# A two-layer graph attention kernel: a new table of places, transfers modelled kind by kind, and one sum kept in a slot of `x`

## The chip, the cores and the metric

The kernel runs on one core of one Trainium2 chip. The metric is the device time of one execution in microseconds (us). The time before is the median of three executions, 2783.31 us (2777.88 to 2784.37). A core has a TensorE (PE, matrix products), a VectorE (DVE), a ScalarE (ACT), a GpSimd (POOL) and a SyncE (SP). Each runs its own list of instructions strictly in order and waits at the head of that list for the semaphores of other engines. Here SP does nothing but issue transfers (DMAs), POOL issues the transfers that add to what is in their destination, and ACT and DVE share the elementwise work.

## The reference, cut to what matters

For each of 32 graphs of 512 nodes with 512 features, the layer normalizes the features, applies a relu, and runs two graph attention layers: the first with 4 heads of 256 features, the second with one head of 512. The result is added to the input.

```python
def gat_layer(x, mask, W, a_src, a_dst, bias, concat):
    B, N, _ = x.shape
    H, F = a_src.shape
    xl = (x @ W).reshape(B, N, H, F)
    asrc = jnp.einsum('bnhf,hf->bnh', xl, a_src)
    adst = jnp.einsum('bnhf,hf->bnh', xl, a_dst)
    e = jax.nn.leaky_relu(asrc[:, :, None, :] + adst[:, None, :, :], NEG_SLOPE)
    e = jnp.where(mask[..., None], e, NEG_INF)
    attn = jax.nn.softmax(e, axis=1)
    out = jnp.einsum('bsdh,bshf->bdhf', attn, xl)
    ...

h = jnp.maximum(_layernorm(x, axis=-1), 0.0)
# gat: layer 1 (concat, elu), layer 2 (mean over one head)
x = x + gat(adj, h, W1, att_src1, att_dst1, b1, W2, att_src2, att_dst2, b2)
```

All of it is float32. For one graph the products with weights are 512x512 by 512x1024 (layer 1) and 512x1024 by 1024x512 (layer 2), and the attention products are 512x512 by 512x256 for each of four heads and 512x512 by 512x512 for the second layer.

## The kernel before, in words

**Products.** Each of the four products of a graph (`project1`, `gather1`, `project2`, `gather2`) is cut into 2x2 blocks and done with seven block products in place of eight. That needs sums of blocks of the left and of the right operand, which DVE makes (`sums`, `sums1`, `sums2`), and sums of the seven results, which ACT and DVE make when they take a result out of its PSUM bank. There are eight banks. A block product is one job on PE of two or four matmuls of 256 to 258 columns. One of the seven products of `project1` (number 5, `SMALL`) is itself cut in seven, with matmuls of 129 columns (`step`). A matmul in float32 shows as two matmul records in the trace.

In `sums` the four sums of the left operand are `s1`, `s2`, a sum in place, and `s4`. In `project1`, `s4` has a tile of its own, `hs4`, which product 3 of all four quarters of the result reads. In `gather1` of the last turn (order `SINGLY`) `hs4` holds the fourth sums too. `x` has four slots (`xs`): a graph's four input tiles lie there from their load to the end of `norm_turn`, and `sums2` takes three of them for right operands of `gather2`.

**Turns.** The main loop has 31 turns. Turn i does the first attention product of graph i+1, the second layer's softmax and attention product of graph i, `project1` and the first layer's softmax of graph i+2, `project2` of graph i+1, and loads and normalizes graph i+3. Before the loop lie the loads of weights, their scores (`scores1`), graph 0 and `project1` of graph 1.

**A softmax in this kernel** goes through DRAM twice for each pair of heads. `columns` computes per-node scores; `spread` turns them on DVE, writes 4 KB to DRAM (`das<-as`), and reads them back onto all partitions (`as<-das`, 512 KB). `first` reads `as` with one ACT instruction (`l<-as,z`) for each of four tiles, adds the transposed mask on DVE, takes exponentials on ACT, and spreads the sums the same way (`drr<-rr`, `rr<-drr`). `second` builds the probabilities in `p`, has POOL add the mask from DRAM (`p<-dm`), and takes exponentials on ACT.

**What sets the order.** No instruction is emitted when its line of the kernel runs. `Program.add` records a job with its engine, its cost in us, the keys it reads and writes, and for a transfer a size. `Program.ranks` gives every job a rank from the table `PLACES` (in hundredths of a us, one number for every job ahead of the loop, of one turn and of the last turn; later turns add the PE work of a turn). `Program.order` then plays five engines in order and two transfer queues ("wires", SP's and POOL's): whenever an engine is free it takes, of the jobs whose inputs the model holds to be ready, the one with the lowest rank. The order found is the order in which each engine's instructions are emitted; costs, sizes and places have no other effect. In this model a transfer starts `DMA_LEAD` after its issue, takes its size in us, slowed by a share in `SHARED` when both queues are busy, and is known to have landed `DMA_TAIL` later.

```python
if len(busy) == 2:
    speed["SP"], speed["POOL"] = self.SHARED.get(jobs[wires["SP"][0][0]][4], (0.4, 0.6))
...
    release(j, lambda s: event + self.DMA_TAIL[which])
```

**Where the recorded lines are.** The helpers that record (`act`, `dve`, `dma`, `accumulate`, `pe`) have one line each, so the profile shows nearly all of ACT at L495, DVE at L498, SP at L501, POOL's transfers at L506 and PE at L512. Tiles tell the work apart.

Of the kernel before, what the change touches and what calls it, by code (L numbers as in the profile page):

```python
# [10 lines left out]
F32 = mybir.dt.float32  # L11
# [8 lines left out]
P = 128  # L20
# [24 lines left out]
class Banks(Slots):  # L45
# [314 lines left out]
def tile_gat(  # L360
# [616 lines left out]
    M = N // 2  # L977
# [713 lines left out]
```

## Time and profile before

| what | value |
|---|---|
| median of three executions | 2783.31 us |
| lowest and highest | 2777.88 and 2784.37 us |
| the profiled execution's own time | 2778.11 us |
| its span, first to last instruction | 2776.3 us |
| PE busy | 2747.9 us |
| DVE busy | 2561.7 us |
| ACT busy | 2224.7 us |
| POOL busy | 321.7 us |
| share of 16 DMA engines' span, SP's queue and POOL's | 42.4% and 25.1% |

The span is the time from the first to the last instruction; 1.8 us of the profiled execution's time lie around it. Busy time is the union of an engine's instructions; matmuls overlap one another in the records, since the next one starts while the one before drains. The views of waits give, for an engine and a tile, what ended its idle time, in us in total, how many times, and the longest. A timeline row gives start, length, engine and tile, how many instructions were merged, and in brackets the idle time before it.

### The profile page before, as it was taken

How to read it: one execution, taken by the hardware profiler on the slowest of the kernel's cores; microseconds unless marked ns; L12 is line 12 of the kernel's file. 1: busy time of each engine (PE TensorE's matmuls, PEld its weight loads, DVE VectorE, ACT ScalarE, POOL GpSimd, SP SyncE). 2: the span in 40 equal slices, each digit the busy share in tenths (PEclk: the TensorE clock that was granted, in tenths of full speed). 3: DMA queues.
4: the chain of work that ended last, by engine and by line, in shares of the span. 5: the costliest groups of instructions: out<-in, count | busy, mean ns of one | idle time of the engine just before them, and what ended most of it. 6: DMA issues, size and time to landing. Idle time of an engine off the chain costs nothing. (4 is left out here: it accounts for less than half of the span.)

```text
span 2776.3 us, 42499 instructions
## 1 busy us (share of the span) xinstructions
PE 2747.9 (99%) x12924; PEld 2375.5 (86%) x12924; DVE 2561.7 (92%) x6732; ACT 2224.7 (80%) x4907; POOL 321.7 (12%) x356
## 2 busy tenths in 40 slices
PE   7999999999999999999999999999999999999999
PEld 6688888888888888888888888888888888888887
DVE  7899999999999999999999999999999999999996
ACT  5978788788887787887888877878778788778783
POOL 0101111101111111111011111111111111101110
PEclk9999999999999999999999999999999999999999
DMA  7757766767666767667686666766666766677663
GB/s 224 182 146 180 199 177 173 199 172 201 175 179 180 187 177 199 178 175 195 170 206 174 175 184 174 191 190 176 178 194 172 203 173 172 194 168 201 165 159 117
DMA packets 375865, 502.15 MB, mean 181 GB/s; under 512 B 222804, under 2 KB 227668, under 8 KB 375636
## 3 DMA queue, kind: packets, MB, share of 16 engines
q1 hardware_dynamic: 329844, 332.68, 42.4%
q0 software_dynamic: 45792, 166.74, 25.1%
q8 instruction: 103, 1.69, 0.3%
q14 instruction: 126, 1.03, 0.1%
HBM read 316.41 MB, written 51.31 MB: 132 GB/s over the span
## 5 line engine op out<-in xcount | busy, mean ns | idle before, releaser
L512 PE MATMUL mm<-w_sb,hs 128*128 128x257 f32 (+3 forms) x2908 | 675.8, 368 | 12.8 <-ACT xl L495 5.9
L512 PEld LDWEIGHTS mm<-w_sb,hs 128*128 128x128 f32 x2908 | 540.1, 190 | 93.3 <-ACT xl L495 8.9
L506 POOL DMA_DIRECT2D p<-dm x314 | 273.5, 877 | 2328.9 <-DVE p L498 1095.2
L512 PE MATMUL mm<-w_sb,ht 128*128 128x258 f32 x2112 | 522.8, 382 | 0.1
L512 PE MATMUL mm<-p,xl 128*128 128x258 f32 (+1 forms) x1984 | 493.1, 383 | 1.5 <-ACT mm L495 0.8
L512 PE MATMUL mm<-w_sb,h 128*128 128x257 f32 x2056 | 487.2, 379 | 0.2 <-ACT mm L495 0.2
L498 DVE SCALAR_TENSOR_TENSOR p<-rr,z 128x512 f32<-128x512 f32 (+1 forms) x636 | 447.4, 742 | 4.6 <-DMA rr<-drr 4.4
L512 PEld LDWEIGHTS mm<-w_sb,ht 128*128 128x128 f32 x2112 | 394.5, 190 | 58.0 <-issue 0.7
L495 ACT ACTIVATE p<-p,z 128x512 f32<-128x512 f32 (+1 forms) x636 | 428.2, 713 | 19.6 <-DVE p L498 13.0
L512 PEld LDWEIGHTS mm<-w_sb,h 128*128 128x128 f32 x2056 | 389.3, 189 | 58.2 <-ACT mm L495 0.6
L512 PEld LDWEIGHTS mm<-p,xl 128*128 128x128 f32 x1984 | 365.1, 190 | 61.2 <-issue 5.5
L495 ACT ACTIVATE l<-l,low 128x512 f32<-128x512 f32 x516 | 369.7, 717 | 1.9 <-DVE low L498 1.6
L495 ACT ACTIVATE l<-as,z 128x512 f32<-128x512 f32 x516 | 353.2, 715 | 14.6 <-DMA as<-das 14.3
L498 DVE CUSTOM_DVE_ANT_1 l<-l,mt 128x512 f32<-128x512 f32 x516 | 345.3, 688 | 18.1 <-ACT l L495 12.7
L495 ACT ACTIVATE xl<-mm 128x258 f32<-128x258 f32 (+2 forms) x748 | 274.2, 376 | 81.5 <-PE mm L512 80.2
L495 ACT ACTIVATE mm<-mm 128x257 f32<-128x257 f32 (+2 forms) x498 | 169.8, 345 | 203.3 <-PE mm L512 108.4
L495 ACT ACTIVATE h<-mm,b_sb 128x256 f32<-128x256 f32 (+1 forms) x504 | 227.8, 473 | 121.5 <-PE mm L512 121.0
L512 PE MATMUL mm<-t,hs 128*128 128x258 f32 (+1 forms) x992 | 254.7, 380 | 0.0
L512 PEld LDWEIGHTS mm<-t,hs 128*128 128x128 f32 x992 | 183.6, 190 | 24.0 <-DVE xl L498 0.4
L495 ACT ACTIVATE xr<-h 128x512 f32<-128x512 f32 x256 | 159.7, 625 | 45.5 <-DVE h L498 42.8
L512 PE MATMUL mm<-xl,p 128*128 128x258 f32 (+3 forms) x752 | 190.0, 388 | 0.0
L498 DVE TENSOR_TENSOR xl<-xl,mm 128x258 f32<-128x258 f32 x372 | 155.7, 420 | 36.2 <-PE mm L512 31.7
(137 smaller groups left out, 3752.6 us busy)
## 6 DMA issues: line engine op xcount, KB each, us to landing
p<-dm POOLq DMA_DIRECT2D x314, 512.0 KB, 5.0
rr<-drr SPq DMA_DIRECT2D x159, 512.0 KB
x<-in_x_dram SPq DMA_DIRECT2D x129, 256.0 KB
adj<-in_adj_dram SPq DMA_DIRECT2D x128, 256.0 KB
as<-das SPq DMA_DIRECT2D x64, 512.0 KB
t<-in_x_dram SPq DMA_DIRECT2D x124, 256.0 KB
out_dram<-t SPq DMA_DIRECT2D x124, 256.0 KB
dm<-m SPq DMA_DIRECT2D x64, 256.0 KB
```

The costliest lines, as they stand in the source:

```text
L495: prog.add("ACT", cost, reads, writes, lambda: nc.scalar.activation(*a, **k))
L498: prog.add("DVE", cost, reads, writes, lambda: f(*a, **k))
L506: lambda: nc.gpsimd.dma_start(to, at, accum_op=OP.add), size,
L512: f(*a, **k)
```

## The change

Six things change; the jobs, their engines and their instructions stay the same.

1. All of `PLACES` is replaced.
2. A transfer's lead, tail and the two shares of speed are looked up by its size in a table `KIND` (`MASK` for POOL's), in place of one lead and tail for each queue and a table of shares.
3. Sizes of transfers in the model change: loads of `x` and masks 0.93 to 0.76, loads of weights 0.93 to 0.89 (and 1.5 to 1.78 for a block of the second weights), stores 0.77 to 0.70, POOL's additions 2.35 to 2.14, transposes 1.25 to 0.97, mask stores 0.80 to 0.73, the 4 KB writes 0.10 to 0.25, the spread rows 1.16 and 2.32 to 0.79 and 2.28.
4. The cost of a small product of 129 columns goes from 129/593 to 129/576 us.
5. The tile `hs4` is gone. In `sums` of `project1`, `s4` takes a slot of `x`, given back when `project1` ends; the four `x` slots so serve eight takers in a turn in place of seven.
6. In the last turn's `gather1`, the fourth sums of all heads take halves of one slot of `x`, given back at its end.

```diff
 PLACES = (
-    -54128, -54128, -54128, -54317, -50216, -53799, -49031, -53371, -49031, -48940, -49031, -48940, -5322, 4139,
...
+    39933, 29566, 31469, 32046, 32674, 28922, 29748, 26576, 30181, 34026,
 )
...
-    DMA_LEAD, DMA_TAIL, AHEAD = {"SP": 0.45, "POOL": 0.42}, {'SP': 1.2, 'POOL': 1.15}, 3.5
-    SHARED = {0.93: (0.31, 0.7), 0.77: (0.43, 0.71), 2.32: (0.75, 0.31), 1.16: (0.75, 0.31), 1.25: (0.35, 0.57)}
+    AHEAD, MASK, OTHER = 3.5, (0.69, 1.16), 0.76
+    KIND = {
+        0.25: (0.65, 0.33, 0.08, 0.89),
+        0.7: (0.18, 0.97, 0.18, 0.84),
+        0.73: (0.14, 1.23, 1.0, 0.59),
+        0.76: (0.91, 0.87, 0.36, 0.59),
+        0.79: (1.9, 0.76, 0.49, 0.45),
+        0.89: (0.65, 1.5, 0.11, 0.87),
+        0.97: (-0.2, 1.07, 0.21, 0.52),
+        1.78: (0.65, 1.5, 0.11, 0.87),
+        2.28: (0.6, 0.96, 0.58, 0.4),
+    }
...
+    def kind(self, j):
+
+        if self.jobs[j][0] == "POOL":
+            return self.MASK
+        return self.KIND.get(self.jobs[j][4], self.KIND[self.OTHER])
...
-                speed["SP"], speed["POOL"] = self.SHARED.get(jobs[wires["SP"][0][0]][4], (0.4, 0.6))
+                speed["SP"], speed["POOL"] = self.kind(wires["SP"][0][0])[2:]
...
-                release(j, lambda s: event + self.DMA_TAIL[which])
+                release(j, lambda s: event + self.kind(j)[1])
...
-                wires[e].append([j, free[e] + self.DMA_LEAD[e], jobs[j][4]])
+                wires[e].append([j, free[e] + self.kind(j)[0], jobs[j][4]])
...
-    hs4 = sbuf.tile([P, KQ, N // 2], F32, name="hs4")
...
-    XLOAD, STORE, MASKS, TURN, MASK_OUT, SMALL_ONE = 0.93, 0.77, 2.35, 1.25, 0.8, 0.1
-    ROWS = {4: 1.16, 8: 2.32}
+    XLOAD, WLOAD, STORE, MASKS, TURN, MASK_OUT, SMALL_ONE = 0.76, 0.89, 0.7, 2.14, 0.97, 0.73, 0.25
+    ROWS = {4: 0.79, 8: 2.28}
...
-            s4 = (hs4, [("hs", 2, 0), ("hs", 2, 1)]) if kh == KQ and at == 0 else s2
+            s4 = s2
+            if kh == KQ and at == 0:
+                xk, xt = xs.take()
+                s4 = xt[:, : KQ * M].rearrange("p (k m) -> p k m", m=M), [xk]
...
+            if place is None:
+                left["own"] = xk
...
-                akeys + bkeys + ([tk + (1,)] if q == 1 else []), [bk], w / 593,
+                akeys + bkeys + ([tk + (1,)] if q == 1 else []), [bk], w / 576,
...
+        xs.give(left["own"])
...
-        ahead = {h for h, n in order[:2]}
+        ahead, apart = {h for h, n in order[:2]}, None
+        if order is SINGLY:
+            xk, xt = xs.take()
+            apart = xk, xt[:, : 2 * M].rearrange("p (i f) -> p i f", i=2)
+            for i in range(2):
+                prog.alias(xk + (i,), [xk])
...
+        if apart:
+            prog.alias(xk, [xk + (i,) for i in range(2)])
+            xs.give(xk)
```

Built, both programs hold the same instructions on each engine. On PE a job moves by at most 17 places in the order, most by four or fewer; on DVE most move by ten or fewer.

More of the change, by code (lines that the diff above doesn't have):

```diff
@@ L594, in weights1 @@
                     dma(
-                        XLOAD, (), [("w1", ix, k)], w1_sb[:, ix, k, :, 2:],
+                        WLOAD, (), [("w1", ix, k)], w1_sb[:, ix, k, :, 2:],
                         w1[row : row + P, :].rearrange("p (j c f) -> p c j f", j=H // 2, c=2)[:, c],
@@ L604, in scores1 @@
                 dma(
-                    0.75, (), [vk + ("v", a, j)], bc[:, 2 * a + j, :],
+                    XLOAD, (), [vk + ("v", a, j)], bc[:, 2 * a + j, :],
                     bass.AP(tensor=v.tensor, offset=v.offset + j * 2 * FH, ap=[[0, P], [1, 2 * FH]]),
@@ L631, in weights2 @@
             dma(
-                1.5, [("ht", 0, 0)], [("w2", ix)], w2_sb[:, ix, :, :M],
+                2 * WLOAD, [("ht", 0, 0)], [("w2", ix)], w2_sb[:, ix, :, :M],
                 w2[r * HF // 2 : (r + 1) * HF // 2, c * DO // 2 : (c + 1) * DO // 2].rearrange(
@@ L646, in weights2 @@
             lk, bc = ts_.take()
-            dma(0.75, (), [lk], bc, rows_of(v[0], P))
+            dma(XLOAD, (), [lk], bc, rows_of(v[0], P))
             for (r, c), ix in AT.items():
@@ L1256, in gather1_plain, with sums1 @@
             yield h
-    def sums1(h, pk, p, apart):
+    def sums1(h, pk, p, apart=None):
         def a_block(i, j):
@@ L1279, in sums1 @@
         if apart:
-            s4 = (hs4[:, h % 2, :].rearrange("p (k f) -> p k f", f=P), [("hs", 2, h % 2)])
+            s4 = (apart[1][:, h % 2].rearrange("p (k f) -> p k f", f=P), [apart[0] + (h % 2,)])
         t1, t2 = (
@@ L1317, in gather1 @@
         blocks, bank = {}, {}
-        ahead = {h for h, n in order[:2]}
+        ahead, apart = {h for h, n in order[:2]}, None
[4 more added lines that the diff above has]
+                prog.alias(xk + (i,), [xk])
         for h in sorted(ahead):
-            blocks[h] = sums1(h, *soft.p[h], order is SINGLY)
+            blocks[h] = sums1(h, *soft.p[h], apart)
         for h, n in order:
             if h not in blocks:
-                blocks[h] = sums1(h, *soft.p[h], order is SINGLY)
+                blocks[h] = sums1(h, *soft.p[h], apart)
             left, right, late, fourth = blocks[h]
```

307 rows, old and new, of the table PLACES are left out of this document.

## The prediction

> **What bounds the kernel now.** I read the first part of the page, then who waited for whom, then windows, then the timeline at the places that the waits name.
>
> ```profile
> span 2776.3 us, 42499 instructions
> PE 2747.9 (99%) x12924; PEld 2375.5 (86%) x12924; DVE 2561.7 (92%) x6732; ACT 2224.7 (80%) x4907; POOL 321.7 (12%) x356
> ```
>
> PE is the bound, and the change takes no matmul away. PE is idle for 2776.3 - 2747.9 = 28.4 us of the span. Only this, and time at a lower clock, can be won by another order; what can be lost has no such lid, since DVE has only 8% of its span free. The next rows say where the 28.4 us lie.
>
> ```profile
> ACT l L495 <- DMA as<-das: 14.3, 15, 4.2
> PE mm L512 <- ACT x L495: 9.5, 1, 9.5
> PEld mm L512 <- ACT xl L495: 9.2, 16, 1.4
> PE mm L512 <- ACT xl L495: 5.9, 11, 1.2
> PE mm L512 <- DVE hs L498: 3.7, 1, 3.7
> PE mm L512 <- ACT mm L495: 3.5, 7, 1.1
> ...
> 2700.25 72.42 PE mm L512 x300
> 2772.69 0.69 DVE t L498
> ```
>
> PE waits 9.5 us for the first normalized tile, 3.7 us once for sums by DVE (`hs`), and 5.9 + 3.5 us for ACT to take results out of banks. The last 72 us are PE without a wait, and the end (2776.3 - 2772.7 = 3.6 us) is the last add and store. First tile and end stay: 28.4 - 9.5 - 3.6 = 15.3 us can go.
>
> ```profile
> 44.40:55.00 10.60, 5.89 (x20) 4.49 (x19) 8.47 (x30) 6.15 (x17) 0.00 (x0) 0.67 0.98 266
> 55.00:60.00 5.00, 5.00 (x19) 4.21 (x18) 3.77 (x20) 2.31 (x8) 0.00 (x0) 0.68 0.31 107
> 600.00:1100.00 500.00, 499.67 (x2379) 436.82 (x2379) 468.77 (x1221) 412.91 (x911) 60.65 (x66) 1.00 0.68 183
> 1600.00:2100.00 500.00, 497.52 (x2368) 434.58 (x2367) 466.12 (x1211) 408.04 (x906) 59.03 (x64) 1.00 0.68 181
> ```
>
> In these windows the first number after the length is PE's busy time, then PEld, DVE, ACT and POOL, then the granted clock. The turns lose 0.3 to 2.5 us in 500. At 44 to 60 us the granted clock drops: (1 - 0.67) x 10.6 + (1 - 0.68) x 5 = 5.1 clock-us missing, that is some 10 us at half clock.
>
> **The change part by part.**
>
> *The costs, sizes, leads and shares* run in no instruction. They act only through the order, with `PLACES`; their own cost is nothing.
>
> *The start.* These rows show the one long wait, on PE, DVE and SP.
>
> ```profile
> 44.02 1.14 PE L512 MATMUL mm<-w_sb,ht 128*128 128x258 f32 x4
> 48.87 2.09 PE L512 MATMUL mm<-w_sb,hs 128*128 128x258 f32 x4 [3.71 <-DVE hs L498]
> 55.07 1.93 PE L512 MATMUL mm<-w_sb,ht 128*128 128x258 f32 x4
> 11.38 0.43 DVE L498 SCALAR_TENSOR_TENSOR xr<-w_sb,p 128x256 f32<-128x256 f32 x1 [0.81 <-DMA p<-in_L_gnn_att_dst_dram]
> 43.96 0.42 DVE L498 SCALAR_TENSOR_TENSOR xr<-w_sb,t 128x256 f32<-128x256 f32 x1 [1.65 <-DMA w_sb<-in_L_gnn_W_dram]
> 44.65 1.23 DVE L498 TENSOR_TENSOR w_sb<-w_sb 128x1032 f32<-128x1032 f32 x1
> 48.13 0.68 DVE L498 TENSOR_TENSOR hs<-hs,ht 128x512 f32<-128x512 f32 x1
> 37.83 1.13 SPq L501 DMA_DIRECT2D w_sb<-in_L_gnn_W_dram  x1
> ```
>
> DVE stood 1.65 us for the second weights, then made a sum of first weights (1.23 us), and only at 48.13 the sum that PE waited for. In the new order the 1.23 us sum stands ahead of that wait and fills it; the second weights are issued ahead of one adjacency pair, a mask store and a transpose that they followed; and, counted in the built orders with each instruction's length from the trace, 1.84 us of DVE work leaves the stretch ahead of the sum against 1.27 us that enters it. That is up to 1.65 + 0.6 = 2.2 us earlier. Against it, the bias `b1`, 1024 elements of 4 bytes, is now loaded as the tenth transfer, ahead of four blocks of weights, and DVE's one instruction on it stands ahead of four scores that the first product needs. No row shows the landing of `b1`. The nearest are two 4 KB writes:
>
> ```profile
> SPq L501 <- DMA das<-as: 121.0, 65, 4.9
> SPq L501 <- DMA drr<-rr: 141.1, 75, 4.3
> ```
>
> They take 1.9 us each on the mean, 4.9 at most; it could also land under the wait for `p` (11.38). So 0 to 4.9 us; as it follows `p`, I take 1.5, nearest the means. Queued behind the waiting instruction are those scores, so PE's first products start 1.5 us later. PE has slack there: it stood 3.7 us at 48.87. The sum then comes at about 48.1 + 1.5 - 2.2 = 47.4 or a little later, and PE reaches it 1.5 us later, so its wait is 1 to 3 us in place of 3.7. Net 0 to 1 us won by the wait.
>
> The clock is worth more. Four matmuls of 258 columns began 48.87 us after a pause of 3.71 us and ran at half pace: 1.93 us for four at 55.07 against 1.14 at 44.02. Ten us at half clock cost about 5 us of PE work, less the waits inside: I take 4. If the pause is short enough the drop goes; a pause of 1 to 3 us stands nearer to 3.71 than to the waits of 1.4 us and less that left the clock at 1.00, so I count it at half. Start: -2.5 us, with ends -7 (both won) and +4 (`b1` at 4.9 us, drop stays).
>
> [...]
>
> *The turns.* Nearly all the waits for `xl` are one place: product 3 of `project1`'s second half takes the bank that ACT's copy of a small product frees. One instance:
>
> ```profile
> 1876.95 0.39 PE L512 MATMUL mm<-w_sb,hs 128*128 128x129 f32 x2
> 1877.17 0.39 PE L512 MATMUL mm<-w_sb,hx 128*128 128x129 f32 x2
> 1878.26 1.03 PE L512 MATMUL mm<-w_sb,ht 128*128 128x258 f32 x4
> 1879.13 0.39 PE L512 MATMUL mm<-wx,hs 128*128 128x129 f32 x2
> 1880.76 1.14 PE L512 MATMUL mm<-w_sb,hs 128*128 128x258 f32 x4 [1.24 <-ACT xl L495]
> 1877.97 1.95 ACT L495 ACTIVATE l<-as,z 128x512 f32<-128x512 f32 x3 [1.41 <-DMA as<-das]
> 1879.83 0.61 ACT L495 ACTIVATE xr<-h 128x512 f32<-128x512 f32 x1
> 1880.35 0.36 ACT L495 ACTIVATE xl<-mm 128x258 f32<-128x258 f32 x1
> 1871.37 0.33 SPq L501 DMA_DIRECT2D as<-das  x1
> ```
>
> ACT waits 1.41 us for `as` to land, does three activations (1.95 us) and an `xr`, and only then the copy. In the new order the third activation, 1.95 / 3 = 0.65 us, stands behind the copy, and PE does another small pair, 1877.17 - 1876.95 = 0.22 us, between. That is 0.87 us more room. The mean of these waits is 9.2 / 16 = 0.58 us, the longest 1.4, so I count nearly all as gone: PE -5.9, and as each shows 1.03 - (1879.13 - 1878.26) = 0.16 us less than PE loses, since a matmul starts while the one before drains, -8.
>
> Against it: the spread whose landing this is stands behind 2.5 us of newly placed DVE work and ahead of 1.3 us that it followed, so it starts 1.2 us later, and two loads of `x` (256 KB each) are now issued ahead of `as`, while an `rr` (512 KB) that was right ahead of it goes out earlier. The landing is later by something between 0 and 1.2 us; I take 0.5, as the bytes queued ahead are fewer. 0.87 - 0.5 leaves 0.4 us more room than before: half of the waits stay away for certain. Then other places: of the places where PE had under 1.2 us to spare I counted PE work and DVE or ACT work ahead of each in both orders: most gain room, five end near zero, none falls below by more than 0.1 us. I take the turns at -5 us, ends -10 and +18 (below).
>
> *`s4` in a slot of `x`.* The DVE sum is the same. What waits is a load: the first `x` tile of the next graph now follows the last product 3 of `project1`, some 37 us later in the turn. Behind it in SP's queue stands a `drr` write that was issued 5 us later still, so nothing queues. Its first reader on DVE has been moved back too, leaving about 3.8 us (estimate, by DVE work between). From issue to use `as` (512 KB) took 1877.97 - 1871.37 = 6.6 us and the 4 KB writes 1.9; a 256 KB load lies between, 4.2. The cover is DVE's free 33 us in 500 of the windows; I cost it at nothing. Uncovered it would be 0.4 us a turn.
>
> *The last turn's slot and the end.* No PE wait stands in the last 72 us, so nothing can be won; 0, within 2 us.
>
> *Sum.* -2.5 - 5 + 0 = -7.5 against the profiled execution's 2778.11 us (its span and 1.8 us): 2770.6. The median shown is 5.2 us above that execution. What it is made of no row shows; late landings at the place above are the likeliest, and these have more room now, so I carry over 2 us: **2772.5 us**, 0.4% under 2783.31. What a measurement of this kernel can tell from no change is about 0.3%, 8.3 us.
>
> **The rivals.**
>
> *The waits move (within 0.3%).* ACT stays behind the same landing, other copies wait in place of the ones mended, and the clock drops as before. For it: five places end near zero room; DVE is 92% busy. Turns 0 to -3, start 0: 2775.5 to 2783, say 2779.
>
> *`as` lands later (slower).* If its landing moves by the whole 1.2 us or more and queues behind both `x` loads, it outgrows the 0.87 us of room. It decides from 0.9 us on: beyond that every turn, not every second one, waits, since 29 turns have one order. At 1.5 us late: 0.6 us x 29 = 17, less nothing won: 2783 + 14 = 2797. For it: 15 ACT waits on `as` already, up to 4.2 us. Against: fewer bytes ahead.
>
> *No drop of the clock and all waits gone.* -7 - 10 = -17: 2761 to 2766. It needs the pause well under the 3.71 us that set the drop off. [...]
>
> **How the numbers follow.** Forecast 2772.5 with 0.35 and the clean case with 0.10: faster 0.45. Waits that move: same 0.34. Late `as` 0.13, and a start hurt by `b1` together with some of it 0.08: slower 0.21. Range 2763 to 2794; it leaves a tenth at each side. The forecast's own range is 2764 to 2775.
>
> **What would show it.** PE's waits on `xl` under 2 us in all; `as` waits on ACT no more than 14.3 us; PE's wait for `hs` near 45 us under 3 us and its clock at 1.00 at 44 to 60 us; the first product of 258 columns at about 14.5 us in place of 12.97; DVE waits for `x` under 5 us. I am wrong if PE's idle time is above 28 us, or if a new releaser of PE appears with over 5 us.

## The result and the profile after

The changed kernel takes 2800.67 us (median of four executions, 2799.22 to 2808.05), the kernel before 2780.65 us in the same comparison. The ratio is 1.0076, with a 95% interval of 1.0053 to 1.0100: the change makes the kernel 0.8% slower. The forecast was 2772.5 us, and the time lies 6.7 us over the upper end of its range. The profiled execution is the slowest of the four (2808.05 us), so that single numbers of its trace may be some us high; run 2 below has the same order and serves as a second trace of it.

The head of the page of the changed kernel:

```profile
span 2806.3 us, 42461 instructions
PE 2765.7 (99%) x12924; PEld 2370.9 (84%) x12924; DVE 2546.8 (91%) x6732; ACT 2221.4 (79%) x4907; POOL 319.7 (11%) x356
```

Who waited for whom, rows that answer to those of before (us in total, times, longest):

```profile
ACT l L511 <- DMA as<-das: 133.7, 61, 4.1
...
PEld mm L528 <- ACT xl L511: 32.9, 46, 2.4
...
ACT p L511 <- DMA p<-dm: 24.3, 40, 3.1
...
DVE p L514 <- DMA rr<-drr: 21.2, 22, 3.0
...
PE mm L528 <- ACT xl L511: 16.7, 25, 2.0
...
PE mm L528 <- ACT x L511: 9.6, 1, 9.6
...
PE mm L528 <- ACT f L511: 2.3, 9, 0.3
...
DVE stats L514 <- DMA x<-in_x_dram: 2.2, 2, 1.9
```

PE is still the bound; its idle time rose from 28.4 to 2806.3 - 2765.7 = 40.6 us. ACT's wait for the read-back `as` rose from 14.3 us in 15 places to 133.7 us in 61, nearly all of the 64 reads. Windows of the same trace, with the columns as before (length, then PE, PEld, DVE, ACT, POOL, granted clock, DMA share, GB/s):

```profile
44.40:55.00 10.60, 7.16 (x38) 5.76 (x37) 10.60 (x44) 9.18 (x26) 0.00 (x0) 1.00 0.82 273
55.00:60.00 5.00, 4.40 (x22) 3.39 (x21) 5.00 (x26) 4.08 (x10) 0.00 (x0) 1.00 0.76 201
600.00:1100.00 500.00, 495.20 (x2331) 427.11 (x2330) 455.08 (x1195) 407.22 (x899) 58.52 (x64) 1.00 0.69 179
1600.00:2100.00 500.00, 495.51 (x2343) 429.03 (x2342) 459.29 (x1205) 399.63 (x888) 57.17 (x63) 1.00 0.70 180
```

The drop of the clock at 44 to 60 us is gone (1.00 against 0.67 and 0.68). In the turns PE does 2331 and 2343 matmul records in 500 us, where it did 2379 and 2368.

PE's idle time does not show all of that, since a matmul that starts late while its forerunner drains looks busy (in the trace after, the pair of 129 columns at 50.42 us is 0.39 us long, and the next pair starts 0.22 us after it). So one more number is counted from each trace, here called *lost in the turns*: for every product of PE from 134 us to the last turn, the time from its start to the next one's, less the spacing of undisturbed matmuls (0.216 us for 256 and 257 columns, 0.217 for 258, 0.110 for 129), added up. It is 24.6 us before and 57.8 us after (53.6 in run 2). Two traces of the same turns differ by some 4 us: 57.8 and 53.6 here, 24.6 and the 28.7 of run 7. Outside the turns the change wins: 11.9 to 10.7 us lost before 62 us, 2.7 to 0.9 us from 62 to 134.

How one turn goes, on SP, DVE and ACT (start, length, what ended the idle time):

```profile
1053.11 0.37 ACT L511 ACTIVATE xl<-mm 128x258 f32<-128x258 f32 x1
1053.38 0.72 ACT L511 ACTIVATE l<-l,low 128x512 f32<-128x512 f32 x1
1054.08 0.38 ACT L511 ACTIVATE xl<-mm 128x258 f32<-128x258 f32 x1
1054.98 0.21 DVE L514 STREAM_TRANSPOSE as<-z 128x32 f32<-128x32 f32 x1
1055.22 0.51 SPq L517 DMA_DIRECT2D das<-as  x1
1055.83 0.39 SPq L517 DMA_DIRECT2D x<-in_x_dram  x1
1056.87 0.33 SPq L517 DMA_DIRECT2D as<-das  x1
1057.63 0.37 ACT L511 ACTIVATE mm<-mm 128x257 f32<-128x257 f32 x1 [2.06 <-DVE t L514]
1061.58 1.34 ACT L511 ACTIVATE l<-as,z 128x512 f32<-128x512 f32 x2 [3.58 <-DMA as<-das]
```

This is the *second* pair's read-back. The copy at 1054.08 finishes the scores that the spread needs. Its product was done 7.2 us earlier (mean of the turns); in the order before the copy came 5.4 us after its product, and now it stands behind more softmax work. So the transpose comes 1.7 us later in the turn than before, the `as` read 1.2 us later, and ACT, which had no wait at this place in any turn, stands 3.4 us in each: 95.0 of its 133.7 us. The first pair, at which the prediction looked, gives 33.0 us (8.0 before).

Not all of the 95.0 us is new idle time of ACT. Right ahead of this read ACT copies a result (`mm<-mm`, at 1057.63 above) for which it waits on DVE; this row stands in the two traces, before first:

```profile
ACT mm L495 <- DVE t L498: 93.0, 29, 3.3
...
ACT mm L511 <- DVE t L514: 59.2, 28, 2.2
```

In the order before, the read had landed 1.4 us before ACT was done there (mean of 28 turns by the read's semaphore; 0.6 us at the least). Now DVE's result comes earlier, ACT is done there 3.1 us earlier in the turn, and the read lands 1.7 us later. So a part of ACT's wait only moved from the copy to the read: ACT begins on the read 0.3 us later in the turn than before.

### The profile page after: what moved, and what is told of

It is laid out like the page before. It is cut to its first block, busy times and chain, and to the rows that moved or that the text cites. A ratio compares the mean times of both kernels' runs of the same rounds, so it can differ in the third digit from the quotient of the medians.

```text
span 2806.3 us, 42461 instructions
## 1 busy us (share of the span) xinstructions
PE 2765.7 (99%) x12924; PEld 2370.9 (84%) x12924; DVE 2546.8 (91%) x6732; ACT 2221.4 (79%) x4907; POOL 319.7 (11%) x356
## 5 line engine op out<-in xcount | busy, mean ns | idle before, releaser
L528 PE MATMUL mm<-w_sb,hs 128*128 128x257 f32 (+2 forms) x2404 | 540.9, 364 | 1.4 <-ACT xl L511 1.3
L528 PE MATMUL mm<-p,xl 128*128 128x258 f32 (+2 forms) x1984 | 506.3, 384 | 0.9 <-DVE p L514 0.5
L528 PEld LDWEIGHTS mm<-w_sb,hs 128*128 128x128 f32 x2404 | 445.2, 190 | 64.5 <-ACT mm L511 2.5
L511 ACT ACTIVATE l<-as,z 128x512 f32<-128x512 f32 x516 | 359.0, 714 | 133.9 <-DMA as<-das 133.7
L528 PEld LDWEIGHTS mm<-w_sb,ht 128*128 128x128 f32 x2112 | 387.7, 190 | 75.9 <-DVE xl L514 14.2
L511 ACT ACTIVATE l<-l,low 128x512 f32<-128x512 f32 x516 | 368.5, 716 | 15.5 <-DVE low L514 15.2
L511 ACT ACTIVATE xl<-mm 128x258 f32<-128x258 f32 (+2 forms) x748 | 265.5, 376 | 77.1 <-PE mm L528 75.5
L511 ACT ACTIVATE h<-mm,b_sb 128x256 f32<-128x256 f32 (+1 forms) x504 | 235.0, 474 | 93.7 <-PE mm L528 93.0
L514 DVE TENSOR_TENSOR xl<-xl,mm 128x258 f32<-128x258 f32 x372 | 152.7, 411 | 41.2 <-PE mm L528 20.8
```

Of the source, the lines that this page charges most:

```text
L511: prog.add("ACT", cost, reads, writes, lambda: nc.scalar.activation(*a, **k))
L514: prog.add("DVE", cost, reads, writes, lambda: f(*a, **k))
L528: f(*a, **k)
```

## The experiments

Three theories. **Theory 1:** the read-backs `as` land later, ACT stands behind them, and the results it then takes out of banks are late for PE. **Theory 2:** `s4` in a slot of `x` costs waits. **Theory 3 and 4:** the new order itself leaves results (3: copies on ACT; 4: results of ACT and DVE alike) no room before PE wants them, wherever the reads land.

Most runs move steps of the order and nothing else. `(k, r)` means: in 28 of the 31 turns (all but the first and the last two), step k goes right ahead of step r on its engine's list; the dependences stay, but for the reads of runs 16 to 18.

```diff
     def emit(self):
-        for j in self.order():
+        for j in self.moved():
             self.jobs[j][3]()
```

All runs in one table. *Tight* counts the products of the turns (of 2632 that take a result of another engine) whose last such result was ready less than 0.1 us before PE could have started them, or later. Each of the last three columns comes from one trace. Runs 1 and 12 to 18 leave out part of the computation, as their expectations say.

| run | ratio to before (95%) | lost in the turns, us | tight | ACT on `as`, us |
|---|---|---|---|---|
| before | 1 | 24.6 | 59 | 14.3 |
| after | 1.0076 (1.0053 to 1.0100) | 57.8 | 134 | 133.7 |
| 1 read from a fixed place | 1.0072 (1.0043 to 1.0100) | 45.8 | 118 | 102.4 |
| 2 `s4` in its own tile | 1.0104 (1.0077 to 1.0131) | 53.6 | 140 | 130.1 |
| 3 spreads and reads earlier | 1.0066 (1.0043 to 1.0088) | 42.5 | 127 | 59.3 |
| 4 two copies earlier | 1.0087 (1.0067 to 1.0107) | 51.6 | 130 | 128.3 |
| 5 before, reads later | 1.0088 (1.0073 to 1.0104) | 51.9 | 75 | 40.5 |
| 6 25 moves | 1.0158 (1.0135 to 1.0182) | 71.8 | 290 | 45.8 |
| 7 new start, old turns | 1.0007 (0.9998 to 1.0016) | 28.7 | 59 | 14.3 |
| 8 16 moves | 1.0137 (1.0115 to 1.0158) | 73.6 | 234 | 130.6 |
| 9 before, third activation moved | 0.9998 (0.9988 to 1.0008) | 25.6 | 86 | 15.2 |
| 10 before, five moves | 1.0018 (1.0007 to 1.0030) | 33.4 | 82 | 15.3 |
| 11 18 moves | 1.0054 (1.0037 to 1.0071) | 47.1 | 170 | 52.2 |
| 12 after, ACT lighter | 1.0075 (1.0052 to 1.0098) | 39.8 | 107 | 126.9 |
| 13 after, DVE lighter | 1.0056 (1.0037 to 1.0075) | 38.0 | 65 | 123.3 |
| 14 before, ACT lighter | 1.0000 (0.9985 to 1.0015) | 21.3 | 28 | 10.7 |
| 15 before, DVE lighter | 1.0015 (1.0005 to 1.0026) | 25.6 | 66 | 9.8 |
| 16 after, reads far ahead | 1.0010 (0.9999 to 1.0021) | 33.5 | 103 | 20.8 |
| 17 as 16, DVE lighter | 0.9986 (0.9975 to 0.9997) | 29.2 | 55 | 21.3 |
| 18 before, reads far ahead | 0.9954 (0.9939 to 0.9970) | 18.0 | 47 | 3.2 |

**Runs 1 and 2: the reads' source, and the slot.**

```diff
+            src = bass.AP(tensor=dr.tensor, offset=dr.offset, ap=[[0, P], [n * P, rows], [1, n * P]])
+            if through in (das,):
+                sb = notes[len(prog.jobs) % 4][:, :]
+                src = bass.AP(tensor=x.tensor, offset=x.offset, ap=[[0, P], [n * P, rows], [1, n * P]])
...
-                ROWS[rows * n], [dk], [ok], o[:, :rows, : n * P],
-                bass.AP(tensor=dr.tensor, offset=dr.offset, ap=[[0, P], [n * P, rows], [1, n * P]]),
+                ROWS[rows * n], [dk], [ok], o[:, :rows, : n * P], src,
```

> The changed kernel, its order untouched. Every read-back `as` takes the same 512 KB from a fixed place in DRAM instead of the rows that the spread has just written (the rows are still written), and the spread's 32 columns go through a tile of their own, so that the read no longer waits for its write: the attention scores are made from other numbers, so this part of the computation is left out. The read goes out some 2 us earlier. Theory 1 (the read-backs `as` of both pairs land later, ACT stands behind them, 133.7 us in place of 14.3, and everything that ACT does afterwards is late): ACT's waits on `as` fall under 60 us, PE's waits on `xl` fall from 49.6 to under 20 us, and the time falls by 15 to 28 us, to 2773 to 2786. Theory 2 (`s4` in a slot of `x`): no change, 2795 to 2806. Theory 3 (places of result copies on ACT and of the mask sums, whatever lands when): under 8 us faster, 2793 to 2802.

Time 2795.39 us. The read did not go out 2 us earlier: in SP's list two residual loads that wait for free `t` tiles (first pair) and an `x` load (second pair) stand ahead of it. It went out 0.1 and 0.7 us earlier, and ACT's waits fell from 133.7 to 102.4 us only. So this run did not make the condition that it was to test; run 16 does.

```diff
+    hs4 = sbuf.tile([P, KQ, N // 2], F32, name="hs4")
...
-                s4 = xt[:, : KQ * M].rearrange("p (k m) -> p k m", m=M), [xk]
+                s4 = hs4, [xk]
```

> The changed kernel with its order untouched, but the fourth sum of `ht` is written to a tile of its own, as before the change, so that no instruction waits for it through a slot of `x`. Theory 2 (the slot of `x` costs): 10 to 20 us faster, 2780 to 2790. Theories 1 and 3 (the order costs): the same within 5 us, 2796 to 2806, with ACT's waits on `as` still at 120 to 145 us.

Time 2805.15 us, the waits on `as` unchanged: theory 2 falls. In this order, the slot of `x` costs nothing that the run can tell.

**Runs 3 and 4: bring spreads, or two copies, forward.**

```diff
+    MOVES = ((160, 227), (163, 227), (165, 355), (291, 186), (312, 194), (315, 194), (317, 406))
```

Steps 160 and 163 are the first pair's doubling of scores and its transpose, 312 and 315 the second pair's, 165 and 317 the two `as` reads, 291 the copy at 1054.08 above.

> The changed kernel with eight moves of the order undone in every turn, and nothing else: on DVE the doubling and the transpose of the first pair's spread go ahead of a 0.41 us subtraction and a 0.68 us one, those of the second pair ahead of a row minimum and three scalings; on ACT the copy of the second half's third product of the last row, ready 7 us before it is made, goes ahead of the softmax work that it followed; on SP the `as` read goes ahead of the two residual loads (first pair) and of one `x` load (second pair). Both reads go out about 1.2 us earlier than in the changed kernel. Theory 1: ACT's waits on `as` fall from 133.7 by about 60 us (1.1 us in each of 56), PE loses 8 to 20 us less, 2781 to 2793. Theory 3: no more than 5 us faster, 2796 to 2801.

The list has seven moves; the expectations say eight here and below, and their sums of moves are one too high. Time 2795.23 us; waits of this run:

```profile
ACT l L533 <- DMA as<-das: 59.3, 42, 3.1
...
PEld mm L550 <- ACT xl L533: 13.0, 23, 1.5
...
PE mm L550 <- ACT xl L533: 5.6, 11, 1.1
```

The waits on `as` and on `xl` fall by more than half and the loss in the turns from 57.8 to 42.5 us (53.6 in the second trace of the same order), all of it where theory 1 puts it: product 3 behind the first pair's read loses 1.4 us in place of 10.4, and a product of project2, after the second pair's, 0.3 in place of 9.0 (4.2 in run 2's trace). But 42.5 is not 24.6, and the time is only 0.1 to 0.4% of the kernel before better than that of the changed order (1.0076, and 1.0104 in run 2). Another part is left.

```diff
+    MOVES = ((441, 342), (435, 338))
```

> The changed kernel with two moves on ACT in every turn: the two copies of project2 whose banks the product that waited 8.7 us in six turns takes (one is ready at about 36 us of the turn and made at 43.8) go 7 us and 0.7 us earlier. Theory 3 in its narrow form (this place costs what it shows): 6 to 9 us faster, 2791 to 2795. Theory 1: the copies are late because ACT is late; with them moved this place goes but the same lateness appears at another one: 0 to 6 us faster, 2795 to 2801, ACT's waits on `as` unchanged.

Time 2800.12 us: project2's product loses 1.7 us in place of 9.0 (4.2 in run 2's trace), and the time does not follow. Within what the runs can tell, theory 3 in its narrow form is not supported.

**Run 5: theory 1 in the kernel before.**

```diff
+    MOVES = ((51, 160), (227, 160), (41, 160), (372, 312), (419, 312), (355, 165))
```

> The kernel before with six moves in every turn: on DVE three subtractions ahead of the first pair's spread and a scaling and a 1.18 us sum ahead of the second pair's, so that both transposes come 1.3 to 1.5 us later, as late as in the changed kernel; on SP one residual load goes ahead of the first pair's `as` read. ACT's order and PE's order are those of before. Theory 1 (late read-backs of `as` are what costs the changed kernel its time): ACT's waits on `as` rise from 14 to 80 us or more, PE loses 10 to 20 us more in the turns, 10 to 20 us slower than before. Theory 4 (the new order gives many products of PE no room: twice as many take a result that is ready less than 0.1 us before they could start, 134 in place of 59 in the turns, and the late reads make only some of them): waits of ACT rise in the same way, but the time by 0 to 8 us, since the places of this order have room.

Time 2805.6 us, 1.0088: late reads, with the steps of DVE and SP that were put ahead of them, make the kernel before as slow as the changed one. That is some 25 us, more than either theory gave (10 to 20 and 0 to 8).

```profile
ACT l L517 <- DMA as<-das: 40.5, 31, 4.2
...
PEld mm L534 <- ACT xl L517: 34.6, 32, 2.0
...
PE mm L534 <- ACT xl L517: 28.2, 31, 1.8
```

A window of the turns in the same trace:

```profile
600.00:1100.00 500.00, 493.82 (x2344) 431.44 (x2343) 462.92 (x1201) 408.53 (x900) 59.37 (x64) 1.00 0.68 181
```

ACT's waits rose by less than expected (in this order ACT comes later to the second pair's read and still need not wait), but the first pair's is enough. The read goes out 0.7 us later in the turn, ACT starts on it 0.6 us later, and product 3 loses 31.9 us where it lost 8.1. That is 0.85 us more in each of 28 turns.

**Runs 6, 8 and 11: give single products room.** Run 8 has these sixteen moves, run 6 these with those of runs 3 and 4, run 11 nine in their place: eight of the sixteen, and step 101 ahead of 204.

```diff
+    MOVES = ((85, 51), (153, 51), (101, 203), (128, 203), (125, 58), (123, 59), (119, 102), (35, 102), (235, 90), (285, 377), (181, 188), (281, 188), (28, 47), (279, 97), (273, 177), (264, 162))
```

> The changed kernel with 26 moves in every turn: the eight that bring the spreads and their reads forward, the two of project2's copies, and sixteen more on DVE and ACT, each of which takes the result that a product of PE waits for ahead of one or two instructions that nobody waits for yet. PE's own order is untouched. Theory 4: the products of the turns with less than 0.1 us of room fall from 134 to under 80, PE's loss in the turns from 54 to 58 us to under 35, and the time by 15 to 25 us against the changed kernel, to within 6 us of before. Theory 1: not much more than the eight moves gave, 0 to 5 us under them, 2790 to 2795.

> The changed kernel with only the sixteen moves that give single products room, and the spreads and their reads as late as the change puts them. Theory 4: 6 to 14 us faster than the changed kernel, with ACT's waits on `as` at 110 us or more. Theory 1: within 4 us of the changed kernel, since ACT stays late and the lateness appears at other products.

> The changed kernel with the eight moves that bring spreads and reads forward, the two of project2's copies, and nine moves in place of the sixteen that went wrong: none of them makes a result later that a product takes with less than 0.5 us of room. Theories 1 and 4 together (half of the loss is the late reads, the rest products that have been left no room for their inputs): PE's loss in the turns falls from 54 to 58 us to 28 to 36 us, 2779 to 2787. Theory 1 alone: no better than the eight moves, 2790 to 2797. If moves of single results only push the lateness to the next place: 2790 to 2810, with other products losing 10 us or more.

Times 2824.59, 2819.46 and 2795.94 us. In runs 6 and 8 neither theory's expectation held; run 11 is hardly better than run 3 (1.0054 and 1.0066), as theory 1 alone had it. The products aimed at lost nothing any more (the one behind step 153: from 1.3 + 2.8 us, its own and the next one's, to 0.2), but results that were put back by 0.3 to 0.9 us became late for others, in all 28 turns: one product went from 0.1 to 11.0 us (run 8), another from 0.4 to 9.1 (run 6), and product 3 from 10.4 to 19.5 (run 8). The tight products rose from 134 to 234 and 290, and the time with them. Moves of single results by hand push the lateness to the next place; they do not tell how much of the loss theory 4 owns.

**Run 7: the new start with the old turns.** The first 674 steps in the new order, the rest in the old.

> The order of the changed kernel for the 674 steps ahead of the first turn (loads, first projection, first graphs) joined to the order of before for all turns and the end, with `s4` in its own tile as before. If the start of the changed kernel is better by what its trace shows (1.2 us less lost before 62 us, 1.8 us less from 62 to 134 us) and the turns are what costs: 1 to 4 us faster than before. If the loss hangs on the start (the turns run late because they begin in another state): 8 us or more slower than before.

Time 2782.09 us. The start does not carry the loss; the turns do. Nor does it carry a gain:

```profile
44.40:55.00 10.60, 7.16 (x38) 5.77 (x37) 10.41 (x43) 9.14 (x26) 0.00 (x0) 1.00 0.77 263
```

The clock stays at 1.00 there too, and 10.4 us are lost before 62 us in place of 11.9. But 5.1 us are lost between 62 and 134 us in place of 2.7. There PE paused 2.29 us, and the clock went to half for 3.41 us, from 127.78 us on:

```profile
126.90 2.98 PE L598 MATMUL mm<-w_sb,hs 128*128 128x257 f32 x8 [2.29 <-ACT xl L581]
...
126.00:134.00 8.00, 7.10 (x25) 5.92 (x26) 5.28 (x16) 8.00 (x17) 0.00 (x0) 0.79 0.70 176
```

**Runs 9 and 10: the prediction's own step, alone.**

```diff
+    MOVES = ((242, 166), (262, 166))
...
+    MOVES = ((242, 166), (262, 166), (266, 251), (163, 51), (315, 372))
```

The first line is run 9, the second run 10. Step 166 is the third activation on the first pair's read, 262 the copy that product 3 waits for, 266 the small copy after it.

> The kernel before with one step of the prediction done alone: on ACT the third of the three activations on the read-back goes behind the copy that product 3 waits for, in every turn, which gives that copy 0.6 us more room; spreads, reads and everything else are those of before. The place loses 9.9 us in the turns of before, 8.1 at the product and the rest at the next. The step of the prediction is right by itself: 6 to 9 us faster than before, 2770 to 2775. If the place only passes its lateness on: within 2 us of before.

Time 2780.27 us, no change.

```profile
ACT l L517 <- DMA as<-das: 15.2, 19, 4.5
...
PEld mm L534 <- ACT xl L517: 2.1, 8, 0.5
...
PE mm L534 <- ACT xl L517: 0.3, 1, 0.3
...
PEld mm L534 <- ACT mm L517: 21.2, 50, 1.4
```

The wait for `xl` is gone as the prediction had it, and stands at the next product, which takes a bank that ACT frees two steps later: product 3 lost 8.1 us and loses 1.1, the next lost 1.8 and loses 7.0.

> The kernel before with five moves in every turn: the third activation behind the copy (the run above), a small copy of ACT ahead of another result, and on DVE each of the two transposes of the spreads ahead of one instruction that nobody waits for (0.68 and 0.48 us), so that both read-backs of `as` are asked for 0.5 us earlier. Theory 1: PE's loss in the turns falls from 25 to 13 to 17 us, 8 to 12 us faster than before, 2768 to 2773, and faster than both kernels. If an earlier read is worth nothing where the copy has room: as the run above, 2770 to 2775.

Time 2785.18 us. Another bank's copy goes ahead, and the wait moves one place further: 1.6 and 1.1 us at those two, 11.9 us at a third product that had lost 0.1. And the reads were not earlier: the first transpose came 0.6 us sooner, but SP was just issuing a residual load, and the read went out 0.05 us sooner.

**Runs 12 to 15: take load off ACT or DVE.** The first edit is that of runs 12 and 14, the second that of runs 13 and 15.

```diff
-                            0.706, [lk, wk + (0, d)], [lk, wk + (1, d)], e, e, AF.Exp,
+                            0.706, [lk, wk + (0, d)], [lk, wk + (1, d)], e[:, :M], e[:, :M], AF.Exp,
...
-            h1[:, g, :], e, 1.0, h1[:, g, :], op0=OP.min, op1=OP.max,
+            h1[:, g, :P], e[:, :P], 1.0, h1[:, g, :P], op0=OP.min, op1=OP.max,
```

> The changed kernel, order untouched, with ACT's 16 exponentials of `l` in a turn made on 256 of 512 columns (the rest of the softmax sum is left out, and 1 is added ahead of the logarithm so that it stays finite): ACT has some 3.4 us less to do in a turn, DVE and PE the same. Theory 1 (what the products wait for is ACT, which stands behind the reads): PE's loss in the turns falls by more than half, 15 to 25 us faster than the changed kernel. Theory 4 (products without room, most of them fed by DVE): 3 to 10 us faster.

> The changed kernel, order untouched, with DVE's 8 last steps of the activation in a turn made on 128 of 512 columns (that part of the activation is left out): DVE has some 3 us less to do in a turn. Theory 4: the products that DVE feeds get room, and DVE's spreads and row minima come earlier too: 12 to 25 us faster than the changed kernel. Theory 1 in its narrow form (ACT behind landings that the spreads' place on DVE sets, with DVE itself on time): 0 to 8 us faster.

> The kernel before with the same ACT work left out. Its waits are nearly all for one copy right behind the reads, ahead of which no exponential stands: 0 to 5 us faster than before. What is left between this run and the one of the changed kernel with the same work left out is the part of the difference that ACT's load does not explain.

> The kernel before with the same DVE work left out: the spreads go out earlier and the one wait of its turns shrinks, 2 to 8 us faster than before. What is left between this run and that of the changed kernel with DVE lightened is the part that DVE's load does not explain: under 6 us by Theory 4, 15 us or more if the order costs by itself.

Times 2792.07, 2789.06, 2772.87 and 2777.45 us. Less work for ACT leaves the ratio where it was (1.0075); less for DVE gives it 0.2%. ACT still waits 126.9 and 123.3 us for `as`. With the same work left out of both kernels, the changed one stays slower by 1.0075 - 1.0000 = 0.75% (ACT) and by 1.0056 - 1.0015 = 0.41% (DVE). So ACT's load has no part in the difference that these runs show. Whether DVE's has one stays open: 11.6 us between runs 13 and 15 lie between the under 6 and the 15 us or more of the expectation, and the intervals are wide. The waits for `as`, 133.7 us after the change, are by runs 12 and 13 of latency more than of load. With DVE lighter the tight products fall to 65, about as many as before the change, and still 38.0 us are lost, 9.7 of them at product 3 behind the first read.

**Runs 16 to 18: bring the reads forward indeed.** The source as in run 1, so that no read waits for its write, and SP's order:

```diff
+    MOVES = ((165, 89), (317, 316))
...
+    MOVES = ((165, 356), (317, 316))
```

The first line is runs 16 and 17 on the changed kernel, the second run 18 on the kernel before. Step 165 is the first pair's read, 317 the second's.

> The changed kernel with each read-back `as` taken from a fixed place in DRAM, so that it waits for no write (the scores are other numbers, that part of the computation is left out), and now also moved ahead on SP: the first pair's read goes out ahead of an `rr` read, a spread write and two residual loads, the second pair's ahead of a spread write and one `x` load. The orders of PE, ACT, DVE and POOL are those of the changed kernel. The reads go out some 5 us and 4 us earlier and land before ACT comes to them. Theory 1: ACT's waits on `as` fall from 133.7 to under 20 us, the losses at the bank behind the reads (12.7 us) and at project2's product (9.7 us) go, PE's loss in the turns falls from 54 to 58 us to 28 to 38 us, 13 to 22 us faster than the changed kernel. If the late reads are only a sign of something else: less than 6 us faster.

Time 2782.09 us, ratio 1.0010.

```profile
ACT l L539 <- DMA as<-in_x_dram: 20.8, 28, 1.8
...
PEld mm L556 <- ACT xl L539: 8.0, 16, 1.8
...
PE mm L556 <- ACT xl L539: 3.7, 6, 1.4
```

One window of the same trace:

```profile
1600.00:2100.00 500.00, 498.98 (x2368) 434.73 (x2367) 463.03 (x1213) 409.19 (x906) 58.38 (x64) 1.00 0.69 183
```

The reads go out 5.4 and 4.1 us earlier. Product 3 loses 0.1 us in place of 10.4, project2's 0.3 in place of 9.0 (4.2 in run 2's trace), and the time falls by 0.7 to 0.9% of the kernel before (1.0076 and run 2's 1.0104, to 1.0010). No engine's order but SP's was touched, and run 1, with the same source and SP's order as it was, gave 1.0072. So theory 1 holds for this part of the loss.

> The run above with DVE's 8 last steps of the activation in a turn made on 128 of 512 columns as well. If late reads and products that DVE feeds without room are together all of the loss: PE's loss in the turns at 18 to 27 us, the time at or under that of before. If something else is left: over 32 us of loss, 8 us or more slower than before.

> The kernel before with the same reads from a fixed place, moved ahead on SP in the same way. Its waits for the bank behind the read (8 to 10 us) go: 5 to 10 us faster than before. What is then left between this run and the one of the changed kernel with its reads ahead is what the new order costs apart from its reads: 10 us or more by theory 4, under 5 us by theory 1.

Times 2774.61 and 2765.54 us.

```profile
ACT l L523 <- DMA as<-in_x_dram: 3.2, 1, 3.2
...
PEld mm L540 <- ACT xl L523: 1.3, 3, 0.8
```

One window of the same trace:

```profile
600.00:1100.00 500.00, 500.00 (x2384) 437.50 (x2384) 469.12 (x1224) 413.77 (x913) 60.77 (x66) 1.00 0.68 183
```

In the kernel before the same step gains 0.46%, some 12.8 us where 5 to 10 were expected, and PE has no idle time left in the window. Between runs 16 and 18, with the first pair's read out of the way in both, 1.0010 - 0.9954 = 0.56% stays, some 15 us: about that much the new order costs apart from its reads. In the traces it is 33.5 - 18.0 = 15.5 us. Two things blur it: ACT still stands 18.0 us for the second pair's read in run 16, and run 18's trace is the slowest of its five executions. Run 16 has 103 tight products against 47, and with DVE lighter they go to 55 and the time to 0.14% under that of before, though 29.2 us are still lost where the expectation had 18 to 27. So theory 4 owns a part as well: of the change's 0.76 to 1.04%, 0.56% stays when the reads are ahead in both orders. What share each has is not one number: late reads are worth 0.46% in the old order and 0.7 to 0.9% in the new one. That they meet products with less room there is the likely reason, and no run tests it by itself.

## Why the prediction was wrong

**Two steps failed**, both in *The turns*, which were taken at -5 us and lost 33.2 us more (29.0 in run 2's trace). Of this, product 3 has 2.3 us, project2's product 8.7 (3.9 in run 2), and the remaining 22 us lie at other products.

**The first failed step** is the size of one term: "The landing is later by something between 0 and 1.2 us; I take 0.5, as the bytes queued ahead are fewer." At the place it looked at, the read went out 1.0 us later, landed 0.85 us later by its semaphore, and ACT began on it 0.7 us later on the mean, in all 28 turns late. Against 0.87 us of new room this leaves nothing, where the prediction had 0.4. The room won there (the third activation behind the copy) was real: the copy itself comes only 0.1 us later than before, and product 3 loses 10.4 us, where run 5 with about the same lateness and no such room loses 31.9. But product 3 lost 8.1 us before, which the step counted as won, and now loses 2 more.

**The step looked at one of two reads.** The second pair's read has no wait in the trace of before, so no row of waits names it. It landed 1.4 us before ACT came. The order puts the copy that its spread hangs on behind more softmax work, and lets ACT come 3.1 us earlier: 95 of the 133.7 us of ACT's waits are there now, and the loss at project2's product goes when the read comes earlier (runs 3 and 16). Nothing in the prediction counts it.

**A wait that is covered is not a gain.** Even alone and with the reads where they were, the third activation behind the copy gave 0.9998 (run 9). ACT has the same work to do after the landing, and PE takes several of its results in a row; the one put last was late (7.0 us at the next product in run 9, 11.9 us at a third in run 10). The prediction should have followed ACT's list to the next two products.

**The second failed step, and in size the larger, is the room at other places**, taken at nothing: "most gain room, five end near zero, none falls below by more than 0.1 us." The tight products went from 59 to 134; 59 of the 134 took their result late, by up to 2 us. The count had been made with lengths of the old trace and with ACT on time.

**The rival** *`as` lands later* gave 2797 us at a chance of 0.13, and is what happened, with 2800.67. Its condition was wrong, though: it was to decide from 0.9 us of lateness at the first pair. The landing was 0.85 us late and ACT 0.7. The rival charged 17 us to product 3, which lost 2.3 us more; the second pair and the tight products did the rest. That its number came out near is luck.

**The start** was forecast at -2.5 us and lost 1.2 + 1.8 = 3.0 us less in the trace, 1.8 of it after 62 us, of which the forecast did not speak. The first product of 258 columns starts at 14.43 us (14.5 was forecast), and the pause before the sum went:

```profile
48.58 1.14 PE L528 MATMUL mm<-w_sb,ht 128*128 128x258 f32 x4 [1.42 <-ACT mm L511]
51.80 1.14 PE L528 MATMUL mm<-w_sb,ht 128*128 128x258 f32 x4 [0.78 <-ACT xl L511]
54.64 0.49 PE L528 MATMUL mm<-w_sb,hx 128*128 128x129 f32 x2 [1.25 <-DVE mm L514]
```

Three waits of 0.78 to 1.42 us, and the clock stays up: four matmuls take 1.14 us, not 1.93. Before the change it dropped in a pause of 3.71 us. Between the two the runs differ: pauses of 1.47 us (run 12), 1.98 (15), 2.13 (17), 2.29 (7), 2.47 (5) and 2.55 (14) were followed by 3.41 or 6.83 us at half clock, and pauses of 2.06 (run 13) and 2.00 us (after) were not. So a pause within the 1 to 3 us of the prediction cost the clock in some runs and not in others, as its even chance had it. What the drop at 44 to 60 us cost stays open: run 7 loses 1.5 us less before 62 us without it, and a later pause brought it another drop.

**`s4` in a slot of `x`** at 0: right (run 2). DVE waits for `x` 2.2 us (under 5 was forecast). **The end** at 0: right, 5.3 and 4.9 us lost there. PE's waits for `xl` were to be under 2 us and are 16.7 (32.9 at the weight loads); `as` was to stay at 14.3 and is 133.7. By its own last line (PE idle above 28 us) the prediction is wrong.

## What to carry to other kernels

Before a wait is counted as won, follow the engine that was late to the next two or three results it hands over: in run 9, with the landing where it was, the order only moved the wait among them (from 8.1 to 1.1 us at product 3, from 1.8 to 7.0 at the next). Look at every read that lands shortly before its use, those without a wait row too: 1.4 us to spare were gone when both the read and the engine's arrival moved. And in these runs a transfer was only as early as its place in its queue let it be: an earlier producer gave 0.05 us (run 10), an earlier place in the queue, with the wait for its write dropped, 4 to 5 us (run 16).

## What the runs showed of the hardware that was not expected

Products of PE lost time although their input was there when PE came to them. Over the turns of before and after, by the room between the last result's end and the moment PE could start, with products left out whose follower waited itself:

```
room, us        products   lost per product, us (mean)
-0.10 to 0          21      0.21
0 to 0.05           17      0.17
0.05 to 0.10        59      0.10
0.10 to 0.20       192      0.03
0.20 to 0.50       954      0.02
over 0.50         3390      0.01
```

By this table a product lost 0.21 us on the mean where the result came up to 0.10 us late, still 0.10 us with 0.05 to 0.10 us of room, and 0.03 us with 0.10 to 0.20. In the new order losses of 0.04 to 0.2 us, some of them in no row of waits, add up to 20.4 us in the turns, against 4.8 us before the change.

The clock went to half without a wholly idle stretch ahead of it. Ten of the traces (before and runs 5, 7, 9, 10, 12, 14, 15, 17 and 18) have half clock within the run, for 3.41, 6.83 or 10.24 us, that is one, two or three times 3.41. In the 3.41 us ahead of each, PE was busy for 0.01 to 0.50 of the time (0.50 in run 12, 0.33 in run 7, 0.19 in before).

Load and latency were told apart by making an engine lighter: less work for ACT or DVE (in the window of 600 to 1100 us ACT was busy for 394.4 us in run 12 and DVE for 443.8 in run 13, against 407.2 and 455.1 after the change) changed the time by between 0.2% less (run 13) and 0.15% more (run 15), reads that go out 4 to 5 us earlier by 0.46% to 0.9% less.
